# Blocks exchanged on the way back from DRAM instead of transposes on TensorE, earlier loads for the last projection, and fewer mask pieces before the first attention

## The chip, the core and the metric

The kernel runs on one core of a Trainium2 chip. The metric is the device time of one execution in microseconds (us), and lower is better. A core has four engines that matter here: TensorE (PE in the profile, matmuls; PEld is its weight load), VectorE (DVE), ScalarE (ACT), and GpSimd (POOL). SyncE (SP) only issues DMAs in this kernel; POOL issues them too, and a few are issued by ACT. Each of these engines works through its own instructions in a fixed order, and they wait for one another by semaphores. Matmul results go to PSUM, everything else lives in SBUF, and large intermediate arrays go through DRAM.

## The reference

There are N = 3327 nodes with F = 512 features each, and a 0/1 matrix adj of N x N. Four layers follow one another, each as `x = layernorm(x + layer(x, adj))`:

- Layer 0 is graph attention with 8 heads of 64: for every pair (i, j) with adj = 1 the weight is `exp(leaky_relu(f1[i] + f2[j]))`, the weights of a row are divided by their sum, and `h' = attention @ Wh`.
- Layer 1 takes for each node the mean of its first 64 neighbours (a running count along the row of adj cuts the rest off), puts it through a linear map and a leaky ReLU, and adds a second linear map of the node itself.
- Layer 2 is like layer 0 (8 heads of 64), with an ELU at its end.
- Layer 3 is the same with 4 heads of 128.

```
nb_mean = (keep @ X) / max(cnt, 1)             # layer 1, keep: the first 64 neighbours
x = layernorm(x + leaky(X @ W_line.T + b) + where(cnt > 0, leaky(nb_mean @ W_nb.T + b), 0))
attention = softmax(where(adj > 0, leaky_relu(s1[i] + s2[j]), -9e15))   # layers 0, 2 and 3
```

## The kernel before

**Tiles.** The nodes are cut into NT = 26 tiles of P = 128 rows; the last has 127. HALF = 13 tiles are half of them. The mask of adj (transposed) stays in SBUF for the whole kernel as one byte per pair. It is made from 26 x 4 pieces of 128 x 832 int32 (426 KB each, array raw), each turned into bytes by one instruction: on DVE at L558, or on ACT at L557.

**Stages.** In order of time:

1. The first projection (about 0 to 150 us). For each tile of x, `project1` transposes the tile on PE (four 128x128 transposes, L253, into the PSUM tile pt), ACT copies the result to xT (L255), and DVE adds up xsum (L256). `project2` multiplies xT by the weights (pw, L264), ACT copies the head columns (rc, qc, L268) and takes an exp (dc, L265), DVE scales (vt, L270), and a DMA stores v. Beside this, the first `EARLY = 3 * NT + 4 = 82` mask pieces are loaded by SP (L547; the first eight by ACT) and made by DVE. The pieces of the left half of all tiles come first, then the third quarter, then the fourth.
2. The first attention (to about 953 us). For each half of the columns, each of four groups of heads and each tile j, DVE makes the weights t from the mask (L398), ACT makes y from t (L401), and PE multiplies both (po at L421, pd at L373). The remaining mask pieces hang on this loop as `aside`, one step per j: the step loads piece k on SP and makes piece k - 1. Of these pieces, those with k % 5 in (1, 3) are made by ACT, the others by DVE.
3. The first half of layer 1, `sage` (to about 1175 us): the two linear maps of every tile, with z stored in three parts.
4. The mean, the second half of `sage` (to about 1780 us). For each of the 26 output tiles PE adds up 26 x 3 matmuls into acc (L767). Between them PE makes the running counts pk for the next block of two tiles (L735); ACT first puts carried counts into pk (L727) from cy, which POOL loads (L624), and DVE turns pk into the mask kt (L739). When acc is done, DVE and ACT make the finished tile y (L747 to L749, then `norm_rows`: L152 to L161), and SP stores it to the array x2 (L133). The projection of layer 2 for tile y runs inside the matmuls of the following tile, as two jobs: `project1` at step t = 11 and `project2` at t = 17. The tiles y have two buffers, acc has two.
5. The attention of layer 2 (to about 2570 us), then the last projection, in `third` (to about 2722 us): `finish` loads the attention's result h (L126, from hd) and the layer's input xr (from x2), divides (L180), applies the ELU (L185, L191, L192) and normalizes (L152 to L161); then the tile is stored as x3 and goes through `project1` and `project2`. `finish` of a group of two tiles is called one group ahead; h has 6 buffers, and xr has 2. The first group's `finish` runs at the end of the attention before.
6. The attention of layer 3 and the last normalization (to the end).

**What sets the order.** PE's instructions stand in the order in which the program is written. Those of DVE, ACT, POOL and SP are ordered by a scheduler of the build, once and for all; what is wrapped in `keep_in_program_order` stays at its place. A transpose between x2 and xT on DVE works inside blocks of 32 x 32 only; the kernel already uses that at L439, where the following DMAs (L461, hd<-ob) put the blocks at their places in runs of 32 numbers (128 bytes).

Of the kernel before, what the change touches and what calls it, by code (L numbers as in the profile page):

```python
# [7 lines left out]
F32 = mybir.dt.float32  # L8
# [10 lines left out]
P = 128  # L19
# [13 lines left out]
def kernel(  # L33
# [10 lines left out]
    nc = tc.nc  # L44
    N, F = x.shape
    NT = (N + P - 1) // P
    NP = NT * P
    LAST = N - (NT - 1) * P
    FC = F // P
# [20 lines left out]
    ident = const.tile([P, P], F32, name="ident")  # L70
# [45 lines left out]
    x2 = dram.tile([NP, F], F32, name="x2")  # L116
# [45 lines left out]

    def finish_steps(pool, xin, layer, t0, n, hbufs=6, eng=nc.sync):
        H, D = layer.H, layer.D
        ys, xs, steps = [], [], []

        def load():
            for t in range(t0, t0 + n):  # L170
                h = pool.tile([P, F], F32, name="h", bufs=hbufs)
                load_tile(h, hd, t, eng)
                ys.append(h)
                xr = pool.tile([P, F], F32, name="xr")
                load_tile(xr, xin, t, nc.gpsimd)
                xs.append(xr)

        def divide(s):
            h = ys[s]
            nc.vector.tensor_tensor(h.rearrange("p (h d) -> p h d", h=H), h.rearrange("p (h d) -> p h d", h=H),  # L180
                                    rec[:, t0 + s, :H].rearrange("p (h e) -> p h e", e=1).to_broadcast([P, H, D]),
                                    op=ALU.mult)
            if layer.elu:
                e = pool.tile([P, F], F32, name="e")
                nc.scalar.activation(e, h, AF.Exp)  # L185
                xs.append(e)

        def add(s):
            h, xr = ys[s], xs[s]
            if layer.elu:  # L190
                nc.vector.scalar_tensor_tensor(xr, xs[n + s], 1.0, xr, op0=ALU.min, op1=ALU.add)  # L191
                nc.vector.scalar_tensor_tensor(h, h, 0.0, xr, op0=ALU.max, op1=ALU.add)  # L192
            else:
                nc.vector.tensor_tensor(h, h, xr, op=ALU.add)

        steps.append(load)
        for s in range(n):
            steps += [lambda s=s: divide(s), lambda s=s: add(s)]
        steps.append(lambda: norm_rows(pool, ys, t0))
        return ys, steps  # L200

    def finish(*a):
        ys, steps = finish_steps(*a)
        for f in steps:
            f()
        return ys
# [16 lines left out]
    class Layer:  # L223
# [23 lines left out]
            nc.gpsimd.memset(self.sm, 0.0)  # L247


        def project1(self, pool, ps, xt, t):  # L250
            pt = ps.tile([P, FC, P], F32, name="pt")
            for c in range(FC):
                nc.tensor.transpose(pt[:, c, :], xt[:, c * P:(c + 1) * P], ident)  # L253
            xT = pool.tile([P, FC, P], F32, name="xT")
            nc.scalar.copy(xT, pt)  # L255
            nc.vector.tensor_reduce(xsum[:, :, t], xT, AX.X, ALU.add)  # L256
            return xT

# [351 lines left out]
    def sage(first, first_pool, xin, prev, nxt, wsrc, dst):  # L610
        G = 2
        GW = G * P
        blocks = [(b * G, b * GW) for b in range(NT // G)]
        with tc.tile_pool(name="sg_z", bufs=1, reuse_waits="tile") as zp, \
                tc.tile_pool(name="sg_c", bufs=2, reuse_waits="tile") as cyp:

            groups = [(b, t) for b in range(NT // G) for t in range(0, NT, 4)]
# [17 lines left out]
            with tc.tile_pool(name="sa_w", bufs=1, reuse_waits="tile") as wp, \  # L635
# [37 lines left out]
                ahead = first  # L673
                for t0 in range(0, NT, 2):
                    ys, ahead = ahead, finish(fp, xin, prev, t0 + 2, 2, 6, nc.sync if t0 else nc.gpsimd) \
                        if t0 + 2 < NT else None
                    for s, y in enumerate(ys):
                        xT = step1(y)
# [6 lines left out]
            with tc.tile_pool(name="sb_w", bufs=1, reuse_waits="tile") as wp, \  # L685
# [57 lines left out]
                def output(acc, t):  # L743
                    xi = sp.tile([P, F], F32, name="xi")
                    nc.gpsimd.dma_start(out=xi, in_=xid[t * P:(t + 1) * P, :])
                    y = sp.tile([P, F], F32, name="y", bufs=2)
                    nc.vector.scalar_tensor_tensor(y, acc, cnt[:, 1, t:t + 1], bnb, op0=ALU.mult, op1=ALU.add)  # L747
                    nc.vector.scalar_tensor_tensor(y, y, 0.01, y, op0=ALU.mult, op1=ALU.max)
                    nc.vector.scalar_tensor_tensor(y, y, cnt[:, 2, t:t + 1], xi, op0=ALU.mult, op1=ALU.add)  # L749
                    norm_rows(sp, [y], t)  # L750
                    store_tile(dst, y, t, nc.sync)
                    return y

                carry_in(0)
                kts = kept(0, 0) + kept(0, 2)
                jobs = []
                for b in range(len(blocks)):
                    t0, i0 = blocks[b]
                    last = b + 1 == len(blocks)
                    ahead = []  # L760
                    for s in range(G):
                        acc = ps.tile([P, F], F32, name="acc", bufs=2)
                        for t in range(NT):
                            if b == 0 and len(kts) < NT and t % 2 == 0:
                                kts += kept(0, len(kts))
                            for c in range(3):
                                nc.tensor.matmul(acc, kts[t][:, s * P:(s + 1) * P],  # L767
                                                 zs(t, c) if c < 2 else zl[:, t, :],
                                                 start=t == 0 and c == 0, stop=t == NT - 1 and c == 2)
                            if not last and (len(ahead) < 10 and t % 4 == 1 and b > 0 if s == 0 else  # L770
                                             len(ahead) < min(NT, t + 10) and t % 2 == 1):
                                ahead += kept(b + 1, len(ahead))

                            if jobs and (t == 11 or t == 17 and not (last and s == G - 1)):
                                jobs.pop(0)()
                        y = output(acc, t0 + s)
                        held = {}

                        def job1(y=y, t=t0 + s, held=held):
                            held["xT"] = nxt.project1(sp, ps, y, t)  # L780

                        def job2(t=t0 + s, held=held):
                            nxt.project2(sp, bank, wsb, held["xT"], t)
                            if t == HALF - 1:
                                nxt.prepare(sp, 0, "xi", 1)

                        jobs += [job1, job2]
                    kts = ahead
# [5 lines left out]
    def third(first):  # L794
        with tc.tile_pool(name="col3", bufs=1) as cp, tc.tile_pool(name="at_r3", bufs=2, reuse_waits="tile") as rp:
# [3 lines left out]
            with tc.tile_pool(name="p_w", bufs=1, reuse_waits="tile") as wp, \  # L799
                    tc.tile_pool(name="p", bufs=3, reuse_waits="tile") as pp, \  # L800
                    tc.tile_pool(name="p_f", bufs=2, reuse_waits="tile") as fp, \
                    tc.tile_pool(name="p_ps", bufs=2, space=PSUM, reuse_waits="tile") as ps:
                wsb = wp.tile([P, FC, 2, FW + L3.H], F32, name="wsb")
                load_wide(wsb, w3, nc.gpsimd)
                nc.vector.tensor_copy(wsb[:, :, :, FW:], wa[3].rearrange("p c (e h) -> p c e h", e=2))

                def bank(e):
                    return ps.tile([P, 512], F32, name=f"pw{e}")

                pend = None  # L810
                ahead = first
                for t0 in range(0, NT, 2):
                    ys, ahead = ahead, finish(fp, x2, L2, t0 + 2, 2, 6, nc.sync if t0 else nc.gpsimd) \
                        if t0 + 2 < NT else None
                    for s, y in enumerate(ys):
                        t = t0 + s
                        store_tile(x3, y, t, nc.sync)
                        xT = L3.project1(pp, ps, y, t)
                        if pend:
                            L3.project2(pp, bank, wsb, *pend)  # L820
                        pend = (xT, t)
                        if t == HALF + 1:
                            L3.prepare(pp, 0)
                            L3.first_rows = L3.rows(rp, 0, 0)
                            L3.cut(pp, 0)
                L3.project2(pp, bank, wsb, *pend)
                L3.mean(pp, bank, wsb)
# [3 lines left out]
            with tc.tile_pool(name="f3", bufs=2) as fp, tc.tile_pool(name="f4", bufs=1) as gp:  # L831
                g = gp.tile([P, HALF, F], F32, name="g")
# [85 lines left out]
                for qs in (slice(0, cut_), slice(cut_, HALF)):  # L918
# [4 lines left out]
                    for q in reversed(range(qs.start, qs.stop)):  # L923
                        y = g[:, q, :]
# [6 lines left out]
    L0, L2, L3 = Layer(0, 8, False), Layer(2, 8, True), Layer(3, 4, True)  # L931
# [3 lines left out]
    with tc.tile_pool(name="col0", bufs=1) as cp, tc.tile_pool(name="raw", bufs=2) as rawp, \  # L935
# [4 lines left out]
        with tc.tile_pool(name="p_w", bufs=1, reuse_waits="tile") as wp, \  # L940
# [4 lines left out]
                nc.gpsimd.memset(mask[:, NT - 1, :], 0.0)  # L945
            nc.gpsimd.memset(mask[:, :, N:NP], 0.0)
            pieces = [(t, q) for t in range(NT) for q in range(2)] + [(t, q) for q in (2, 3) for t in range(NT)]
            EARLY = 3 * NT + 4
            msteps = mask_steps(rw0, pieces[:EARLY], 5, (), False, 8)

            def load(t):
# [24 lines left out]
            xT = L0.project1(pp, ps, load(0), 0)  # L976
            held = {}
# [5 lines left out]
            for t in range(1, NT):  # L983
                xT = L0.project1(pp, ps, load(t), t)
# [30 lines left out]

        pieces = pieces[EARLY:]
        ends = []
# [65 lines left out]
```

## Time and profile before

Three runs took 3425.46, 3428.16 and 3432.74 us, so the median is 3428.16 us. The profiled execution has a span of 3432.3 us.

| what | busy us | share of the span |
|---|---|---|
| PE | 3295.2 | 96% |
| PE weight loads | 1656.3 | 48% |
| DVE | 2666.0 | 78% |
| ACT | 2374.3 | 69% |
| POOL | 215.1 | 6% |

The share of an engine is a mean over stages which have different limits. A row of the 40 slices shows when an engine is full: each digit is the busy share of one slice of 85.8 us in tenths. In a timeline, a line has the start, the time from the first to the last of the merged instructions, the engine, the line of the kernel, the operation, what it writes and reads, and in brackets how long the engine was idle before it and what ended the wait. Neighbouring instructions of one engine overlap a little, so the cost of one in a full engine is the distance from its start to the next start.

### The profile page before, as it was taken

How to read it: one execution, taken by the hardware profiler on the slowest of the kernel's cores; microseconds unless marked ns; L12 is line 12 of the kernel's file. 1: busy time of each engine (PE TensorE's matmuls, PEld its weight loads, DVE VectorE, ACT ScalarE, POOL GpSimd, SP SyncE). 2: the span in 40 equal slices, each digit the busy share in tenths (PEclk: the TensorE clock that was granted, in tenths of full speed). 3: DMA queues.
4: the chain of work that ended last, by engine and by line, in shares of the span. 5: the costliest groups of instructions: out<-in, count | busy, mean ns of one | idle time of the engine just before them, and what ended most of it. 6: DMA issues, size and time to landing. Idle time of an engine off the chain costs nothing.

```text
span 3432.3 us, 47383 instructions
## 1 busy us (share of the span) xinstructions
PE 3295.2 (96%) x18705; PEld 1656.3 (48%) x18705; DVE 2666.0 (78%) x2571; ACT 2374.3 (69%) x2172; POOL 215.1 (6%) x344
## 2 busy tenths in 40 slices
PE   8799999999999899999989999999998999999997
PEld 7544344444444355555543444444446654455553
DVE  5799999999967443434349999999997766668876
ACT  2388999999943233333338999899997655559985
POOL 3200000000010111111110000000001000000000
PEclk9999999999999999999999999999998999999998
DMA  9732111111043422222220111111116411112211
GB/s 372 279 110 69 51 48 43 53 45 39 26 140 125 127 81 76 71 71 73 70 70 25 43 49 48 53 49 46 32 34 219 160 40 40 42 47 89 82 37 48
DMA packets 225061, 276.62 MB, mean 81 GB/s; under 512 B 45949, under 2 KB 160327, under 8 KB 224840
## 3 DMA queue, kind: packets, MB, share of 16 engines
q1 hardware_dynamic: 192280, 162.21, 14.8%
q0 software_dynamic: 27040, 103.70, 9.6%
q10 hardware_dynamic: 5520, 7.69, 0.7%
q8 instruction: 148, 2.42, 0.3%
q14 instruction: 73, 0.60, 0.1%
HBM read 204.92 MB, written 68.60 MB: 80 GB/s over the span
## 4 chain that ended last, share of the span: by engine, by line
PE 73%; issue 12%; DMA 6%; DVE 4%; ACT 3%; POOL 1%; SPq 0%; POOLq 0%; ACTq 0%; DVEq 0%
PE po L421 49%; PE pd L373 7%; PE acc L767 5%; DVE t L398 3%; PE pw L264 3%; PE pz L655 3%; PE pi L658 3%; DMA raw<-in_adjT_dram 2%; DMA cy<-ctd 2%; ACT y L401 1%; PE pt L449 1%; PE pe L487 1%; DMA r<-rr 0%; POOL cy L624 0%; PE pa L966 0%
## 5 line engine op out<-in xcount | busy, mean ns | idle before, releaser
L398 DVE SCALAR_TENSOR_TENSOR t<-rb,qc,mask 128x1664 f32<-128x1664 f32 x1040 | 1959.0, 1945 | 183.1 <-PE po L421 163.6
L401 ACT ACTIVATE y<-t,bi,sc 128x1664 fp8e4<-128x1664 f32 x1040 | 1770.0, 1766 | 321.7 <-PE pd L373 302.9
L421 PE MATMUL po<-t,vj 128*64 128x448 f32 (+3 forms) x8320 | 1912.8, 521 | 24.4 <-DVE t L398 24.2
L421 PEld LDWEIGHTS po<-t,vj 128*64 128x64 f32 (+1 forms) x8320 | 835.0, 148 | 978.1 <-issue 710.6
L767 PE MATMUL acc<-zs,kt 128*128 128x512 bf16 x1352 | 404.7, 381 | 0.0
L767 PEld LDWEIGHTS <-kt 128*128 128x128 fp8e4 x2028 | 199.3, 98 | 246.0 <-issue 9.6
L264 PE MATMUL pw<-wsb,xT 128*128 128x264 f32 (+1 forms) x1248 | 302.7, 398 | 9.6 <-DVE vt L270 5.1
L727 ACT CAST pk<-cy 128x512 f32<-128x512 bf16 x169 | 98.4, 587 | 287.1 <-DVE kt L739 234.0
L264 PEld LDWEIGHTS pw<-wsb,xT 128*128 128x128 f32 x1248 | 241.5, 197 | 55.9 <-ACT xT L255 6.0
L373 PE MATMUL pd<-y,sden 128*32 128x448 fp8e4 (+1 forms) x4160 | 259.4, 342 | 8.2 <-ACT y L401 8.2
L767 PE MATMUL acc<-zl,kt 128*128 128x512 bf16 x676 | 257.5, 381 | 4.6 <-DMA zl<-zd 4.6
L739 DVE SCALAR_TENSOR_TENSOR kt<-pk,mask 128x512 fp8e4<-128x512 f32 x169 | 116.2, 688 | 108.2 <-PE pk L735 107.8
L373 PEld LDWEIGHTS <-sden 128*32 128x32 bf16 x4160 | 117.5, 96 | 160.3 <-issue 137.6
L270 DVE TENSOR_TENSOR vt<-pw,dc 128x256 f32<-128x256 f32 x156 | 59.2, 416 | 136.7 <-ACT dc L265 129.7
L352 POOL DMA_DIRECT2D rb<-r x40 | 21.3, 533 | 1607.9 <-DVE t L398 1593.4
L268 ACT COPY rc<-pw 128x8 f32<-128x8 f32 (+1 forms) x78 | 12.7, 163 | 151.0 <-PE pw L264 151.0
L655 PE MATMUL pz<-wn,xT 128*128 128x512 f32 x208 | 93.7, 593 | 1.2 <-ACT xT L649 1.2
L658 PE MATMUL pi<-wl,xT 128*128 128x512 f32 x208 | 93.5, 592 | 0.0
L558 DVE TENSOR_SCALAR mask<-raw 128x832 fp8e4<-128x832 int32 (+2 forms) x95 | 56.2, 600 | 45.6 <-DMA raw<-in_adjT_dram 45.2
L747 DVE SCALAR_TENSOR_TENSOR y<-acc,cnt,bnb 128x512 f32<-128x512 f32 x26 | 19.5, 751 | 88.5 <-PE acc L767 88.5
L624 POOL DMA_DIRECT2D cy<-ctd x91 | 67.9, 746 | 289.5 <-ACT pk L727 264.8
L256 DVE TENSOR_REDUCE xsum<-xT 128x4 f32<-128x512 f32 x78 | 53.0, 681 | 39.7 <-ACT xT L255 39.3
(175 smaller groups left out, 1738.4 us busy)
## 6 DMA issues: line engine op xcount, KB each, us to landing
vj<-v SPq DMA_DIRECT2D x312, 128.0 KB
rb<-r POOLq DMA_DIRECT2D x40, 832.0 KB, 4.6
raw<-in_adjT_dram SPq DMA_DIRECT2D x67, 416.0 KB
cy<-ctd POOLq DMA_DIRECT2D x78, 256.0 KB, 3.9
h<-hd SPq DMA_DIRECT2D x61, 256.0 KB
v<-vt SPq DMA_DIRECT2D x50, 256.0 KB
hd<-hb SPq DMA_DIRECT2D x48, 256.0 KB
xr<-x POOLq DMA_DIRECT2D x45, 256.0 KB, 3.1
```

The lines of the kernel that those rows point to most:

```text
L264: nc.tensor.matmul(pw[e][:, :FW + H], xT[:, c, :], wsb[:, c, e, :], start=c == 0, stop=c == FC - 1)
L270: nc.vector.tensor_tensor(vt[:, hs, :], pw[e][:, :FW].rearrange("p (h d) -> p h d", d=D), self.dc[:, t, hs].rearrange("p (h e) -> p h e", e=1)
L373: nc.tensor.matmul(pd[c][32 * kk:32 * kk + 32, :w_], lhsT, rhs, start=(kk, c) not in seen, skip_group_check=final is not None, stop=last a ...
L398: nc.vector.scalar_tensor_tensor(t, rb[k], self.qc[:, j, h:h + 1], mask[:, j, i0:i0 + IW], op0=ALU.max, op1=ALU.mult)
L401: nc.scalar.activation(y, t, AF.Sigmoid, bias=self.bi[:, j, h:h + 1], scale=self.sc[:, j, h:h + 1], saturate=False)
L421: nc.tensor.matmul(po[c][k * D:(k + 1) * D, :z - a_], vj[:, j % 2, k * D:(k + 1) * D], ts[k][:, a_:z], start=j == 0, stop=j == NT - 1)
L624: nc.gpsimd.dma_start(out=cy[:, :n, :], in_=ctd[t:t + n, b * GW:(b + 1) * GW] .rearrange("(o t) i -> o t i", o=1).to_broadcast([P, n, GW]))
L655: nc.tensor.matmul(pz, xT[:, c, :], wn[:, c, :], start=c == 0, stop=c == FC - 1)
L658: nc.tensor.matmul(pi, xT[:, c, :], wl[:, c, :], start=c == 0, stop=c == FC - 1)
L727: nc.scalar.copy(pks[k % 2], carry[b, t // 4 * 4][:, t % 4:t % 4 + 2, :])
L739: nc.vector.scalar_tensor_tensor(kt, pk, NEIGHBOURS, mask[:, t:t + 2, i0:i0 + GW], op0=ALU.is_le, op1=ALU.mult, saturate=False)
L767: nc.tensor.matmul(acc, kts[t][:, s * P:(s + 1) * P], zs(t, c) if c < 2 else zl[:, t, :], start=t == 0 and c == 0, stop=t == NT - 1 and c ...
```

## The change

There are three edits.

**The mean.** A finished tile y (all but the last) is stored as before, and then read back from x2 into a new tile yx by four DMAs on SP. Each takes 32 partitions, and the 32 x 32 blocks come exchanged: block (a, b) of each 128 x 128 square lands where block (b, a) was. `project1` then makes xT by one transpose on DVE, which stays at its place in the program, instead of four transposes on PE and a copy on ACT. The jobs move: `project1` of a tile runs at t = 17 of the following tile, and `project2` at t = 11 of the tile after that.

**The last projection.** The loads of `finish` are issued three groups ahead, its other steps one group ahead as before. h has 10 buffers, xr has 6. The loads of the groups at tiles 2 and 4 are issued before the loop; those of the group at tile 2 stay on POOL for h.

**The masks.** EARLY is 5 * 26 / 2 + 3 = 68 instead of 82, so 36 pieces are made during the first attention, not 22.

```diff
-    def finish_steps(pool, xin, layer, t0, n, hbufs=6, eng=nc.sync):
+    def finish_steps(pool, xin, layer, t0, n, hbufs=6, eng=nc.sync, xbufs=None):
...
-                xr = pool.tile([P, F], F32, name="xr")
+                xr = pool.tile([P, F], F32, name="xr", bufs=xbufs)
...
-        def project1(self, pool, ps, xt, t):
-            pt = ps.tile([P, FC, P], F32, name="pt")
-            for c in range(FC):
-                nc.tensor.transpose(pt[:, c, :], xt[:, c * P:(c + 1) * P], ident)
+        def project1(self, pool, ps, xt, t, blocks=False):
             xT = pool.tile([P, FC, P], F32, name="xT")
-            nc.scalar.copy(xT, pt)
+            if blocks:
+                tc.keep_in_program_order(nc.vector.transpose(xT, xt))
+            else:
+                pt = ps.tile([P, FC, P], F32, name="pt")
+                for c in range(FC):
+                    nc.tensor.transpose(pt[:, c, :], xt[:, c * P:(c + 1) * P], ident)
+                nc.scalar.copy(xT, pt)
...
                     store_tile(dst, y, t, nc.sync)
-                    return y
+                    if t == NT - 1:
+                        return y
+                    yx = sp.tile([P, FC, P], F32, name="yx")
+                    for q in range(4):
+                        nc.sync.dma_start(out=yx[32 * q:32 * q + 32].rearrange("p c (g f) -> p c g f", g=4),
+                                          in_=dst[t * P:(t + 1) * P, :].rearrange("(g a) (c q f) -> q a c g f", g=4, q=4, f=32)[q])
+                    return yx
...
-                            if jobs and (t == 11 or t == 17 and not (last and s == G - 1)):
+                            if jobs and (t == 11 and t0 + s > 1 or t == 17):
                                 jobs.pop(0)()
...
-                            held["xT"] = nxt.project1(sp, ps, y, t)
+                            held["xT"] = nxt.project1(sp, ps, y, t, t < NT - 1)
...
                 ahead = first
+                groups = []
+                def load_group(t0):
+                    if t0 < NT:
+                        groups.append(finish_steps(fp, x2, L2, t0, 2, 10, nc.gpsimd if t0 < 4 else nc.sync, 6))
+                        groups[-1][1].pop(0)()
+                for t0 in (2, 4):
+                    load_group(t0)
                 for t0 in range(0, NT, 2):
-                    ys, ahead = ahead, finish(fp, x2, L2, t0 + 2, 2, 6, nc.sync if t0 else nc.gpsimd) \
-                        if t0 + 2 < NT else None
+                    ys = ahead
+                    load_group(t0 + 6)
+                    if groups:
+                        ahead, steps = groups.pop(0)
+                        for f in steps:
+                            f()
...
-            EARLY = 3 * NT + 4
+            EARLY = 5 * NT // 2 + 3
```

## The prediction

> **What bounds the kernel now.** I read the page's busy shares and slices, then the waits of each of the three places that the change touches, then their timelines.
>
> ```profile
> PE 3295.2 (96%) x18705; PEld 1656.3 (48%) x18705; DVE 2666.0 (78%) x2571; ACT 2374.3 (69%) x2172; POOL 215.1 (6%) x344
> PE   8799999999999899999989999999998999999997
> DVE  5799999999967443434349999999997766668876
> DMA  9732111111043422222220111111116411112211
> ```
>
> PE fills nearly every slice, but the places differ: two slices at the start run the DMA engines full, slices 3 to 11 (first attention) have DVE as full as PE, slices 14 to 21 (the mean) have PE alone, and slice 31 (last projection) has everything a little short.
>
> The mean, a timeline of PE and SP (start, length, engine, line, operation):
>
> ```profile
> 1414.46 0.32 SPq L133 DMA_DIRECT2D x<-y  x1
> 1415.85 0.38 PE L767 MATMUL acc<-zl,kt 128*128 128x512 bf16 x1
> 1416.07 0.60 PE L253 MATMUL pt<-ident,y 128*128 128x128 f32 x4
> 1416.50 0.60 PE L767 MATMUL acc<-zs,kt 128*128 128x512 bf16 x2
> ...
> 1439.70 0.32 SPq L133 DMA_DIRECT2D x<-y  x1
> 1439.73 0.66 PE L253 MATMUL pt<-ident,y 128*128 128x128 f32 x4 [0.37 <-ACT y L161]
> ```
>
> PE goes from one matmul into the next; the four transposes take 0.43 us of its order (1416.07 to 1416.50), and the second group waited 0.37 for its tile. So a matmul taken out here is time won.
>
> The last projection, PE and DVE:
>
> ```profile
> 2633.79 0.69 DVE L180 TENSOR_TENSOR h<-h,rec 128x512 f32<-128x512 f32 x1 [2.90 <-DMA h<-hd]
> 2639.71 3.67 PE L264 MATMUL pw<-wsb,xT 128*128 128x260 f32 x16
> 2646.81 1.03 PE L253 MATMUL pt<-ident,h 128*128 128x128 f32 x4 [3.42 <-ACT h L161]
> 2647.63 5.02 PE L264 MATMUL pw<-wsb,xT 128*128 128x260 f32 x16
> 2684.29 0.69 DVE L191 SCALAR_TENSOR_TENSOR xr<-e,xr 128x512 f32<-128x512 f32 x1 [3.06 <-DMA xr<-x]
> ```
>
> and PE's waits between 2600 and 2722 (in all, times, longest):
>
> ```profile
> PE pt L253 <- ACT h L161: 9.6, 4, 3.4
> ```
>
> DVE stands for a load, and some ten us later PE stands for the tile that the load belongs to: 9.6 us in four waits.
>
> The first stage's end and the first attention, DVE:
>
> ```profile
> 143.29 0.59 DVE L558 TENSOR_SCALAR mask<-raw 128x832 fp8e4<-128x832 int32 x1 [1.40 <-DMA raw<-in_adjT_dram]
> 149.69 7.53 DVE L398 SCALAR_TENSOR_TENSOR t<-rb,qc,mask 128x1664 f32<-128x1664 f32 x4
> 228.93 7.53 DVE L398 SCALAR_TENSOR_TENSOR t<-rb,qc,mask 128x1664 f32<-128x1664 f32 x4
> 236.37 0.59 DVE L558 TENSOR_SCALAR mask<-raw 128x831 fp8e4<-128x831 int32 x1
> 236.88 7.53 DVE L398 SCALAR_TENSOR_TENSOR t<-rb,qc,mask 128x1664 f32<-128x1664 f32 x4
> ```
>
> Before 149.69 DVE waits for mask pieces; after it, it runs without a gap (between 150 and 260 it waits 0.4 us in all). There a mask piece costs 0.51 us of DVE (236.37 to 236.88), and nothing hides it.
>
> **What the Trainium skill says.** "VectorE: DVE Perf Modes", The three transpose paths: VectorE transposes inside 32x32 blocks only, TensorE the full 128x128, into PSUM. That is why blocks must be exchanged on the way back, and why the TensorE way carries a ScalarE copy (L255, 585 ns in the mean). "DMA: Bandwidth & Descriptors", Anatomy of one DMA: some 2 us are fixed, mostly the wait until the last byte has landed. The trace fits: 256 KB of xi land in 2.9 us. The same page, Specifications: below 512 B a transfer doesn't reach full rate. The trace agrees: the 128 B runs of hd<-ob go at 102 to 144 GB/s between 2812 and 2820, where the first stage reads at about 400. "TensorE: Matmul & The Clock Gate", Why this matters for your kernels: idle gaps over about 3 us lower the clock. Above, after 3.42 us, the transposes take 1.03 for 0.60 and the projection 5.02 for 3.67, so such a wait costs some 1.8 us more than itself.
>
> **The change, part by part.**
>
> *Mean.* 25 of 26 tiles lose four transposes: 25 x 0.43 = 10.8 us of PE. PE's waits for y there go too (2.4 us in 7 waits, in PE's waits for this stage). Together 13.2. ScalarE loses 25 copies of 0.585, which aren't on the path. DVE gets a transpose instead of nothing: the nearest row is L439, 583 ns for 128x448 from PSUM, so an estimate of 0.66 us for 128x512, in a stage where DVE is 40% busy; it hides under the matmuls as long as its data is there.
>
> Is it there? Each tile adds four loads on SP, 2048 runs of 128 B. SP first waits until the store has landed (3.8 us, the stores of v of the same size) and then issues four (0.32 to 0.84 each). The 6656 runs of one hd<-ob set moved in 8.4 us (2811.4 to 2819.8), 1.26 ns each, so 2048 take 2.6. That is a write; for a read from DRAM the worst row is cb<-ctd, 3328 elements of two bytes, landed after 11.7 us, so 2048 runs take at most 7.2. With 2 us fixed the blocks arrive 3.8 + 1.5 + 2.6 + 2 = 9.9 us after the store's issue; 14.5 at the upper bound. The store comes 6.6 or 9.9 us after the tile's end (acc read at 1407.85, store 1414.46; 1429.76 and 1439.70). So arrival is 16.5 to 19.8, worst 24.4. The transpose stands, in the built order of DVE, behind the last kt of the next tile and ahead of its first y: PE reaches t = 17 after 17 x 0.65 + 8 x 0.22 + 3.56 (the projection, now at t = 11) = 16.4, and the tile ends at about 22.7 (24 periods of y from 1203.65 to 1749.77). DVE may stand there for up to 3.5 us; behind it are xsum and the next y, which wait for PE anyway. The xT is used only at t = 11 of the tile after. No cost, at the worst bound 1 to 2 us on the y chain, which has 20 us of slack in the second acc.
>
> On SP, the stores of v are behind these loads; nobody waits for them in this stage. On the DMA engines (a quarter busy in the mean) the 2.6 us can hold up a carry load (cy, 3.9 us to land), and PE's order can't pass a pk whose copy is late. ScalarE already waits 51 us for cy, of which 5.6 reach PE. Bounds 0 and 25 x 0.5 = 12 us; I take 1. Mean: -12 us.
>
> *Last projection.* The same loads and arithmetic, issued two groups earlier (xr from 2 to 6 buffers, h from 6 to 10). That takes DVE's waits for h and xr (5.7 + 5.2 us between 2600 and 2722), and with them PE's 9.6 us and about 2.5 of slow clock: at most -12. But the static orders change too. At the start ScalarE now does two exp of the next groups and rc, dc, qc of the first projection ahead of the second group's sqrt, and POOL issues the 1 MB of weights ahead of the second group's loads: PE then waits about 3 us for tile 2 (ScalarE: projection ends, 0.2, table 1.28, 0.29, DVE 0.4, 0.8), and wins 1.5 because the first group gets ready sooner. Also DVE needs 3.85 us a tile (from start to start: 5 x 0.6, 0.67 for vt, 0.2) against PE's 3.95, so it has hardly anything in hand, least where prepare and cut add some 4.5. Bounds -12 and +3; I take -7. On POOL all xr loads now precede the rows of the next attention; they are issued by tile 20, some 25 us before these rows are needed: nothing.
>
> *Masks.* Fourteen pieces leave the first stage: 14 x 0.426 MB at about 390 GB/s = 15 us of DMA, but PE allows less. With mask waits the last tiles take 4.65 us, without them 4.0 (as at 34 to 46 us), for four tiles 2.6; and the pieces and waits between 143.3 and 149.2 vanish from DVE: the first L398 comes at about 143.7 instead of 149.69, -6. In the attention 36 pieces stand instead of 22; by the list of those on ScalarE, 22 instead of 13 are DVE's: 9 x 0.51 = +4.6, all on the path. ScalarE gets 5 x 0.98 more, hidden under DVE (it is 90% busy). The loads are on SP among vj, one per step as before. Sum -1.5, bounds -5 and +4.
>
> Sum -12 - 7 - 1.5 = -20.5 us on the traced 3432.3, that is 3412. The three unprofiled runs are 3425 to 3433 with a median of 3428.16, so **3408 us**.
>
> **Rivals.**
> 1. The last projection wins nothing, since DVE and ScalarE take PE's place as soon as loads are early: for it their load of 3.85 a tile and the order at the start; against it that every long PE wait has a DMA wait before it. Then -13.5: 3415.
> 2. The readback disturbs the carry loads, and PE pays 0.4 us a tile: the mean returns only 2 us. For it: PE's slack for a pk is half a microsecond; against: three quarters of the DMA time are free. Total -10: 3418.
> 3. Slower: the 128 B reads are much slower than the writes of that size. From about 22 us after a tile's end, 12 us after the later stores, DVE holds back kt of the next tile, and PE stops at the second pk. Each us more costs 13 us at first (only every other tile has the later store). The 21.7 us that the change else returns are eaten when the blocks land 1.7 us past that limit, about 14 us after the store's issue, where I expect 9.9; at 15 us the sum is 13 x 3 - 22 = +17: 3445.
> 4. The masks only move: attention +4.6, first stage not earlier, because PE is the bound there. Then the sum is -14: 3414.
>
> **How the numbers follow.** This kernel's three runs spread over 0.2%, so 0.2% (6.9 us) is about what a measurement can tell from no change. Forecast as such 0.52 (3400 to 3416); rivals 1 and 4 together 0.20 (3411 to 3419); rival 2 0.10 (3415 to 3424, half of it inside 0.2%); rival 3 0.09; gains beyond 28 us 0.09. Faster 0.82, same 0.09, slower 0.09. The range 3396 to 3424 leaves out rival 3 and half of the largest gains; the likeliest case's own range is 3400 to 3416.
>
> **What would show it.** Mean: 4 instead of 104 matmuls pt<-y, 25 stream transposes near 0.66 us, the period of y from 22.7 down to about 22.2, no DVE wait for yx beyond 4 us, waits PE pk <- ACT pk still near 6. Last projection: no DVE wait for h or xr after the first groups, PE's wait for h below 5 us. First stage: the first L398 near 144, but the end of the first attention only 1 to 2 us earlier than 953. Wrong would be: long DVE waits for yx, PE waits for pk, or a first projection that stands several times for ScalarE.

## The result and the profile after

The changed kernel takes 3411.38 us (median of 4 runs, 3406.59 to 3413.64) against 3429.25 us on the same chip: a ratio of 0.9946, 95% interval 0.9929 to 0.9964, so 18 us faster. Run again later beside the kernel before it took 3409.40 us, ratio 0.9925 (0.9908 to 0.9943). 3408 was forecast, with 3396 to 3424 as the range.

The traced execution spans 3404.9 us (3432.3 before). The page, engines and slices:

```profile
PE 3279.8 (96%) x18605; PEld 1646.2 (48%) x18605; DVE 2676.6 (79%) x2591; ACT 2363.6 (69%) x2152; POOL 214.8 (6%) x344
PE   8899999999999899999989999999998999999997
DMA  9543111111143433333321011111107311112211
```

PE is 15.4 us less busy and has 100 fewer matmuls: 25 tiles by four transposes. DVE has 10.6 us more. The DMA row at the front went from 9732 to 9543, since the mask pieces come a little later, and in the mean (slices 15 to 20) it rose from 2 to 3: the blocks that are read back.

The mean, timeline of SP and DVE (start, length, engine, line, operation):

```profile
1380.21 0.33 SPq L133 DMA_DIRECT2D x<-y  x1
1382.28 2.60 SPq L761 DMA_DIRECT2D yx<-x  x4
1389.18 0.71 DVE L254 STREAM_TRANSPOSE xT<-yx 128x512 f32<-128x512 f32 x1 [1.67 <-DMA yx<-x]
...
1399.91 0.33 SPq L133 DMA_DIRECT2D x<-y  x1
1403.80 2.60 SPq L761 DMA_DIRECT2D yx<-x  x4
1410.19 0.70 DVE L254 STREAM_TRANSPOSE xT<-yx 128x512 f32<-128x512 f32 x1
```

The first of these tiles had its blocks 9.0 us after its store was issued (DVE stood for them, so 1389.18 is when they came); the second tile's were there when DVE asked, 10.3 us after the store. DVE's waits over the whole mean (in all, times, longest):

```profile
DVE xT L254 <- DMA yx<-x: 10.2, 10, 1.8
```

Over those ten tiles the blocks came 7.7 to 9.0 us after the store's issue. The waits don't reach PE: among its own waits from 1175 to 1765 none is for this transpose. In the last projection, PE's waits and the start of its timeline:

```profile
PE pt L258 <- ACT h L161: 4.5, 2, 3.6
```

```profile
2580.08 0.66 PE L258 MATMUL pt<-ident,h 128*128 128x128 f32 x4 [3.63 <-ACT h L161]
2580.58 5.36 PE L268 MATMUL pw<-wsb,xT 128*128 128x260 f32 x16
2586.21 3.67 PE L268 MATMUL pw<-wsb,xT 128*128 128x260 f32 x16
```

Of the long waits for h one is left, the one that the new order makes at the start (3.63, and 1.7 more in the matmuls after it, 5.36 for 3.67). The other 0.9 us of the 4.5 are one short wait. The first attention begins here:

```profile
142.13 7.54 DVE L402 SCALAR_TENSOR_TENSOR t<-rb,qc,mask 128x1664 f32<-128x1664 f32 x4 [0.98 <-PE pw L290]
```

What ends the idle time is now PE's last matmul of the projection, and no mask piece.

**The stages over all traces.** I measured the same landmarks in the trace of every kernel: the first t (start of the first attention), the first `h<-h,rec` after it, the first and last `y<-acc` of the mean, the first transpose of the last projection and the first `po` of the last attention. The kernels below `after` are described under the experiments. Lengths in us:

| Kernel | start of first attention | first attention | mean | last projection |
|---|---|---|---|---|
| before | 149.69 | 803.51 | 563.39 | 130.69 |
| mean_alone | 147.07 | 804.78 | 548.15 | 133.88 |
| shift_alone | 145.97 | 804.31 | 559.46 | 133.43 |
| proj_alone | 145.04 | 804.66 | 563.26 | 122.34 |
| masks_alone | 142.71 | 811.26 | 563.55 | 131.88 |
| after | 142.13 | 807.05 | 546.47 | 124.08 |
| after_again | 142.31 | 808.14 | 548.67 | 123.10 |
| no_mask_edit | 144.46 | 805.33 | 548.69 | 124.79 |
| early_56 | 138.78 | 812.63 | 548.74 | 123.63 |
| no_readback | 142.91 | 808.54 | 547.17 | 124.03 |
| slot_14 | 143.40 | 807.73 | 548.67 | 123.05 |
| slot_11 | 142.90 | 809.26 | 725.03 | 123.58 |
| sage_blocks | 143.97 | 809.86 | 546.95 | 124.63 |
| sage_free | 141.66 | 809.12 | 546.20 | 123.92 |

The table is worth more than a comparison of the first two traces. Five programs with the same first stage (82 pieces) begin their first attention anywhere from 144.46 to 149.69, so the trace of before was the latest of five. The 7.6 us that two traces seem to show there are half a matter of the draw: from the mean of these five (146.4) to the mean of the eight with 68 pieces (142.7) it is 3.7 us.

### The profile page after: what moved, and what is told of

Read it like the earlier page. It is cut to its first block, busy times and chain, and to the rows that moved or that the text cites. A ratio compares the mean times of both kernels' runs of the same rounds, so it can differ in the third digit from the quotient of the medians.

```text
span 3404.9 us, 47272 instructions
## 1 busy us (share of the span) xinstructions
PE 3279.8 (96%) x18605; PEld 1646.2 (48%) x18605; DVE 2676.6 (79%) x2591; ACT 2363.6 (69%) x2152; POOL 214.8 (6%) x344
## 3 DMA queue, kind: packets, MB, share of 16 engines
q1 hardware_dynamic: 245080, 168.77, 16.3%
## 4 chain that ended last, share of the span: by engine, by line
PE 80%; DVE 6%; issue 6%; DMA 5%; ACT 3%; POOL 0%; ACTq 0%; POOLq 0%; SPq 0%; DVEq 0%
PE po L425 49%; PE acc L778 11%; PE pd L377 7%; PE pw L268 4%; DVE t L402 4%; DMA raw<-in_adjT_dram 3%; PE pz L659 3%; PE pi L662 3%; ACT y L405 1%; PE pt L453 1%; PE pk L739 1%; PE pe L491 1%; DMA cy<-ctd 1%; DVE mask L562 0%; DMA cb<-ctd 0%
```

## Experiments

**1. The three parts, each alone.** Each is the kernel before with one part of the diff. For the mean:

```
-            nc.scalar.copy(xT, pt)                      # after four TensorE transposes of y
+            tc.keep_in_program_order(nc.vector.transpose(xT, xt))    # xt: y read back in blocks
-            if jobs and (t == 11 or t == 17 and not (last and s == G - 1)):
+            if jobs and (t == 11 and t0 + s > 1 or t == 17):
```

> The kernel before with the edit of the mean alone (readback in exchanged blocks, VectorE's transposes, the later job slots). Theory: between the first y and the last y the trace of the changed kernel was 16.9 us shorter, and this edit alone brings all of it: 13 to 17 us faster, about 3413 to 3416 us, with the last y some 17 us earlier in the trace and the last projection still 130 us long. Rival A: the readback disturbs the carry loads and the edit pays less than the transposes that leave TensorE: 3 to 7 us faster. Rival B: the 16.9 us came from other conditions that the mask or projection edits made: under 3 us.

Measured: ratio 0.9949 (0.9935 to 0.9964), 17.5 us. The mean is 15.2 us shorter than in the trace of before, and the projection is not shorter (133.88 for 130.69). Rivals A and B fall.

For the last projection:

```
-  ys, ahead = ahead, finish(fp, x2, L2, t0 + 2, 2, 6, ...)
+  ys = ahead
+  load_group(t0 + 6)          # h 10 buffers, xr 6
```

> The kernel before with the edit of the last projection alone (loads three groups ahead, ten h and six xr buffers). Theory: the stretch from the first transpose of the projection to the first matmul of the last attention falls from 130.7 to about 124 us and the kernel is 6 to 7 us faster, about 3422 us. Rival: the attention that follows takes it back (it was 2 us longer in the trace of the changed kernel), or the projection is bound by its engines and not by its loads: under 2 us.

Measured: ratio 0.9965 (0.9952 to 0.9977), 12 us; the interval reaches down to 8. PE's waits for h in the projection:

```profile
PE pt L253 <- ACT h L161: 3.6, 1, 3.6
```

Four waits of 9.6 us in all have become the one at the start. Of DVE's waits for the two loads, those for xr (5.2 us in before, between 2600 and 2722) are gone. Of those for h (5.7 us in four) two are left, of 2.2 us in all here and of 4.3 in the changed kernel, and little of them reaches PE. The stage is 8.3 us shorter than in the trace of before; over the traces of the table, it takes 132.5 us without this edit (four) and 123.7 with it (ten).

A part of that goes back just ahead of the landmark. From the last `po` of the attention before to the first transpose of the projection it is 19.3 us without the edit (19.1 to 19.6) and 21.1 with it (20.6 to 21.7). PE there, in before and then in the changed kernel:

```profile
2587.68 0.47 PE L449 MATMUL pt<-ident,ob 128*128 128x128 f32 x1 [0.72 <-ACT hb L453]
2592.09 1.97 PE L253 MATMUL pt<-ident,h 128*128 128x128 f32 x8 [3.93 <-ACT h L161]
```

```profile
2566.68 0.48 PE L453 MATMUL pt<-ident,ob 128*128 128x128 f32 x1 [3.93 <-ACT hb L457]
2569.33 1.97 PE L258 MATMUL pt<-ident,h 128*128 128x128 f32 x8 [2.17 <-ACT h L161]
```

The first group is ready sooner, but the attention's own copy hb on ACT comes later. From that last `po` to the first `po` of the last attention the edit is worth 6.9 us (151.8 to 144.9). The last attention and normalization take back nothing (710.9 us without, 710.8 with). So the loads were what bound it, and by the stages the gain is the 6 to 7 us that were expected; the timing says more.

For the masks (`EARLY = 3 * NT + 4` to `5 * NT // 2 + 3`, 82 to 68):

> The kernel before with 68 mask pieces in place of 82 ahead of the first attention, nothing else. Theory: the first attention starts 7.5 us earlier and takes 3.5 us longer, because 14 more pieces lie in a stretch that VectorE and ScalarE nearly fill: 3 to 5 us faster, about 3425 us. Rival A (the prediction's own sum): 1.5 us faster. Rival B: pieces only move, and the attention takes back all of it: within 1 us.

Measured: ratio 0.9994 (0.9986 to 1.0003), so between 5 us faster and 1 slower: no gain that the timing can tell from nothing. The stages speak for rival B: the start comes earlier, and the attention takes it back (experiment 5).

**2. What the mean is made of.** The same later slots, but TensorE goes on transposing y and nothing is read back:

```
-            if jobs and (t == 11 or t == 17 and not (last and s == G - 1)):
+            if jobs and (t == 11 and t0 + s > 1 or t == 17):
```

> The kernel before with only the job slots of the mean moved (transposes of a tile at step 17 of the next tile and its matmuls at step 11 of the one after); TensorE still transposes y from SBUF and nothing is read back. Theory: the mean's 16.9 us are about 11.3 us of transposes (25 tiles by 0.43 to 0.49 us) and about 5.6 us of TensorE's wait for y at step 11, which the later slot removes; so this kernel is 4 to 7 us faster, the wait of pt for ScalarE's y is near zero, and the pair period is near 44.4 us. Rival A (as the prediction priced it): the wait was worth 2.4 us over all tiles, so 1 to 3 us faster. Rival B: the slot does nothing, and all 16.9 us are the transposes' (they cost more than their rows say): within 1 us.

Measured: ratio 0.9971 (0.9960 to 0.9981), 10 us by the timing, but 3.9 us by the stage that it changes. In the trace the rest lies in the start of the first attention (145.97 for 149.69), which this edit doesn't touch. The timing's interval (7 to 14 us) leaves out 3.9; why it gives more than the stage stays open, and I rest on the stage. 3.9 lies between the theory (4 to 7) and rival A (1 to 3). PE's groups in the mean, of before and then of this kernel:

```profile
L253 PE MATMUL pt<-ident,y 128*128 128x128 f32 x100 | 15.7, 279 | 3.0 <-ACT y L161 2.4
```

```profile
L258 PE MATMUL pt<-ident,y 128*128 128x128 f32 x100 | 15.0, 273 | 0.0
```

The wait is gone. So the later slot gives 3.9 us. Taking the transposes out gives 10.7 to 13.3 more (559.46 to between 546.20 and 548.74 in the seven traces that hold the whole of this edit), 11.8 to their mean of 547.7, against 25 x 0.43 = 10.8. By the timing the difference of the two kernels is 7.5 us, with intervals of 4 and 5 us: too wide to tell these apart.

**3. Is the readback hidden?** The changed kernel without the four loads of a tile; VectorE transposes y itself.

> The changed kernel without the four loads a tile: VectorE transposes y itself within its 32x32 blocks, so what the second layer projects is not the transposed tile; the readback in exchanged blocks is left out, all else stays. Theory: the readback is wholly hidden: the stretch from the first to the last y stays near 548.6 us, and the time is within 2 us of the changed kernel. Rival 2 of the prediction (the loads disturb the carry loads, 0.04 to 0.4 us a tile): 1 to 10 us faster than the changed kernel.

Measured: ratio 0.9932 (0.9918 to 0.9946), 3409.31 us; the mean takes 547.17. That is inside what the kernels with the readback show (546.20 to 548.74). 100 loads of 128 B runs cost nothing that can be seen here, and nothing near the 10 us of the prediction's second rival, which falls.

**4. The deadline of the blocks.** The changed kernel with VectorE's transposes earlier, first by three steps (`t == 17` to `t == 14`), then in the slots of before (`t == 11 or t == 17 and not (last and s == G - 1)`).

> The changed kernel with VectorE's transposes of the tile before at step 14 of the mean's 26 instead of step 17, some 2.4 us earlier. In the changed kernel's trace the blocks were there about 9 us after the store's issue, and VectorE stood at most 1.8 us for them. Theory: now VectorE stands 1 to 4 us at most tiles, and TensorE, which can run ahead by two pk, hardly stands: within 4 us of the changed kernel. Rival 3 of the prediction (each us in which VectorE is held past the slack costs a us of TensorE at 24 tiles): 20 to 60 us slower.

Measured: ratio 0.9927 (0.9915 to 0.9940), the same as the changed kernel. DVE's waits in the mean:

```profile
DVE xT L254 <- DMA yx<-x: 13.7, 11, 2.2
```

Three steps cost DVE 3.5 us in all (it stood at 11 tiles, where the theory had it stand at most of them), and the mean takes 548.67: PE loses nothing.

> The changed kernel with VectorE's transposes at step 11 of the next tile and the projection's matmuls at step 17, which are the slots of the kernel before. By the trace of the changed kernel step 11 comes some 8 us after a tile's end, its y is stored 8 to 9 us after it, and the blocks land some 9 us after that. Theory (rival 3's mechanism, reached from the other side): VectorE stands up to 9 us at every tile with kt behind it, TensorE stops at the second pk and again for xT at step 17, some 3 to 5 us a tile: 60 to 120 us slower than the changed kernel. Rival: TensorE's hold on pk and the kept kt of ten tiles carry it over: under 15 us slower.

Measured: ratio 1.0431 (1.0412 to 1.0451), 149 us slower than before and 174 slower than the kernel without readback beside it. DVE's timeline, PE's timeline, and PE's waits from 1199 to 1930:

```profile
1398.77 0.71 DVE L254 STREAM_TRANSPOSE xT<-yx 128x512 f32<-128x512 f32 x1 [4.74 <-DMA yx<-x]
```

```profile
1399.63 6.24 PE L268 MATMUL pw<-wsb,xT 128*128 128x264 f32 x16 [5.03 <-DVE xT L254]
```

```profile
PE pw L268 <- DVE xT L254: 118.2, 25, 5.7
PE pk L739 <- ACT pk L731: 1.6, 3, 1.0
```

Every tile stands some 4.7 us for xT, and the sixteen matmuls after a wait take 5.9 us on average (5.2 to 6.7, 6.24 in the line above) where the changed kernel's took 3.72 (at 1401.51). 118 + 25 x 2.2 = 173 us, near the 174. The profile also shows the clock that TensorE was granted, as a share of full speed: from 1399.6 to 1402 it is 0.50, and over the mean of the changed kernel 1.00. My theory named the wait for xT, but missed the slow clock and so put the loss at 60 to 120; the place that rival 3 names (PE at the second pk) is wrong: PE waited 1.6 us for pk.

This kernel moves two things: the transposes to step 11, and the matmuls that use them to step 17 of the same tile. The blocks came at 1398.77, and PE, which stood before its step 17, went on 0.86 us later. So PE waited for the load through VectorE, and it would have to wait for it at that step wherever the transpose stood. What transposes at step 11 cost when the matmuls stay a tile later was not run.

**5. The masks again, in the changed kernel.** The whole once more, the whole with 82 pieces, and with 56 (`EARLY = 2 * NT + 4`).

> The changed kernel itself once more, so that the parts can be compared with the whole on one chip. The three parts alone gave ratios of 0.9949 (mean), 0.9965 (last projection) and 0.9994 (masks) to the kernel before. If they add, the whole stands at 0.9908, about 31 us faster than before. If part of it is lost in the combination, or the parts' ratios were high draws, it stays near the 0.9946 of its first run (18 us).

> The changed kernel with 82 mask pieces first, as before; so the mean's and the last projection's edits together. Theory (masks only move: over six traces the first attention starts 4.5 us earlier with 68 pieces and takes 4.9 us longer): within 2 us of the changed kernel. Rival (the landmarks of the first two traces, which gave the mask edit 4 us): 3 to 5 us slower than the changed kernel.

> The changed kernel with 56 mask pieces first in place of 68: the mask edit nearly doubled. Theory (what the first stage gives, the attention takes): first attention starts 4 us earlier still and takes 4 us longer, total within 2 us of the changed kernel. Rival A (the first stage gives 0.54 us a piece, the attention takes 0.25): 3 to 4 us faster. Rival B (the attention's engines are full by now, each further piece costs more than 0.5 us there): 3 to 6 us slower.

Measured, on one chip: 0.9925 (0.9908 to 0.9943) with 68 pieces, 0.9923 (0.9909 to 0.9936) with 82, 0.9932 (0.9917 to 0.9946) with 56. No difference can be told. The start of the first attention in mean_alone (82), masks_alone (68) and early_56:

```profile
147.07 5.67 DVE L402 SCALAR_TENSOR_TENSOR t<-rb,qc,mask 128x1664 f32<-128x1664 f32 x3
```

```profile
142.71 7.54 DVE L398 SCALAR_TENSOR_TENSOR t<-rb,qc,mask 128x1664 f32<-128x1664 f32 x4 [0.98 <-PE pw L286]
```

```profile
138.78 7.54 DVE L402 SCALAR_TENSOR_TENSOR t<-rb,qc,mask 128x1664 f32<-128x1664 f32 x4 [0.98 <-PE pw L290]
```

With fewer pieces the attention starts earlier each time, by about 0.3 us a piece, and takes as much longer or a little more: 804.5 us (the five traces with 82), 808.9 (the eight with 68), 812.6 (the one with 56). So the theory holds at three sizes. As for the whole: the parts' gains sum to 31.6 us, the whole gave some 26 here (0.9925). The intervals (5, 4 and 3 us on the parts, 6 on the whole) are too wide to call that a loss, and the parts share one set of runs of the kernel before, so that an error of that set stands in the sum three times. Summed by stages it is 15.7 for the mean, 6.9 for the projection and 0.7 lost on the masks, 22 in all.

**6. The same idea one stage earlier.** In the stage ahead of the mean PE is full as well, so I tried the exchange there for tiles 6 to 25, finished a group earlier:

```
+                    if yx is not None:
+                        xT = sp.tile([P, FC, P], F32, name="xT")
+                        tc.keep_in_program_order(nc.vector.transpose(xT, yx))
+                        return xT
...
-    ys, ahead = ahead, finish(fp, xin, prev, t0 + 2, 2, 6, ...)
+    ys = queue.pop(0)                                    # the group after it is stored to yd here
+    queue.append(finish(fp, xin, prev, t0 + 4, 2, 7, ...))
...
+    yxs[t0 + 2 + s] = back(t0 + 2 + s)                   # four loads, as in the mean
...
```

Two buffer counts change with it, which no run separates: the stage's tile r1 has one buffer, and h has seven.

> The changed kernel with the same exchange in the stage ahead of the mean: tiles 6 to 25 are finished one group earlier, stored once more, read back in exchanged blocks and transposed by VectorE; TensorE keeps the transposes of tiles 0 to 5. There TensorE goes from matmul to matmul too (30.0 us of 30 between 985 and 1135) and four transposes take 0.44 us of its order; VectorE works 20 to 22 us of 30 and would get 0.70 a tile more. Theory (a matmul taken out of a full TensorE stream is time won as long as the blocks arrive): 20 x 0.44, so the stretch from the end of the first attention to the first y of the mean falls from about 251 to 242 us, and the kernel is 7 to 10 us faster than the changed one, about 3401 us. Rival A: the extra finish of a group ahead and the waits for blocks (VectorE has only some 2 us a tile free) give it back: within 3 us. Rival B: stores and loads on the queue of the stage's other transfers hold up z3 and xi, VectorE stands for their buffers: 5 to 20 us slower.

Measured: ratio 1.0102 (1.0088 to 1.0116), 36 us slower than before and some 61 slower than the changed kernel (no_readback beside it took 3409.31): a loss that is larger than any that I had written down. PE's waits (980 to 1240) and its timeline:

```profile
PE pz L663 <- DVE xT L651: 46.6, 8, 6.3
```

```profile
1074.23 5.45 PE L663 MATMUL pz<-wn,xT 128*128 128x512 f32 x8 [6.02 <-DVE xT L651]
1079.52 3.60 PE L666 MATMUL pi<-wl,xT 128*128 128x512 f32 x8
```

DVE has no wait for the blocks in this stage. Its order has the transposes of two tiles (at 1073.46) right behind the finish of the next group (1070.31 to 1073.44). Without the pin the build puts them elsewhere:

```
-                        tc.keep_in_program_order(nc.vector.transpose(xT, yx))
+                        nc.vector.transpose(xT, yx)
```

> The kernel of the run before (exchange in the stage ahead of the mean for tiles 6 to 25) with VectorE's transposes no longer held behind the whole finish of the group to come: in the built order the transposes of tile k+2 now stand between the first and the last VectorE step of tile k, where before those of k and k+1 stood after the last step of k-1. In the run before TensorE stood 46.6 us in 8 waits for xT and lost its clock. Theory: that order was the whole loss, so those waits vanish and the gain that was meant comes out: the stretch from the end of the first attention to the first y of the mean about 242 us (251 in the changed kernel), the kernel 7 to 10 us faster than the changed one, about 3401 us. Rival A: VectorE's share (0.70 us more a tile, of some 2 us free) or the blocks' arrival is the next bound: within 3 us of the changed kernel. Rival B: the queue of stores and loads holds up z3 and xi: slower by 3 to 20 us.

Measured: ratio 1.0003 (0.9993 to 1.0014), so no faster than before and some 25 us slower than the changed kernel. PE's waits (950 to 1222) and a place of its timeline:

```profile
PE pz L663 <- DVE xT L651: 16.3, 6, 3.5
PE pk L759 <- ACT pk L751: 11.8, 3, 9.8
```

```profile
1081.38 5.40 PE L663 MATMUL pz<-wn,xT 128*128 128x512 f32 x8 [3.50 <-DVE xT L651]
```

The waits for xT fell from 46.6 to 16.3 us but did not vanish: once in two tiles a transpose still stands behind finishing steps that come in one run on DVE (1072.88 to 1080.02 ahead of the transpose at 1080.62). Some 7 us of slow clock follow them. PE's wait for pk at this stage's end is longer, 11.8 us where the changed kernel run again has 5.0, but its wait for zl there (a stored part of z) is shorter, 1.1 for 5.0. The stage takes 270.9 us where it takes 249.6 and 251.4 in the changed kernel. The order was a part of the loss and not the whole. Whether an order written out by hand would give the 8.8 us was not tried. No version that I ran beats the changed kernel; those with 82 and 56 pieces and slot_14 tie with it.

## Why the prediction was right, point by point

- **The total.** 3408 was forecast and 3411 and 3409 came. The sum on the trace was -20.5; the two timings give -18 and -27, the stages -22. That the total fits to 3 us is in part luck: the timings lie 9 us apart, and the mean's gain was put too low while the masks' was put too high. The chances of the cases, added up, give 0.86 for faster and 0.05 for the same, not 0.82 and 0.09.
- **Mean, -12: right in mechanism, two terms mis-sized.** Measured -15.7 (563.4, the mean of three traces in the table, to 547.7, the mean of the seven that hold the whole of this edit). The transposes were put at 10.8 and gave some 11.8. The wait for y was put at 2.4, read from PE's waits; taking it away gave 3.9. The 1 us for disturbed carry loads was not there. Of the 5.6 us that PE was said to wait for pk, one wait of 4.5 stands before the first y; within the mean it is 1.0 in before and 0.7 after.
- **The readback.** Arrival was put at 9.9 us after the store's issue and was 7.7 to 9.0 at the ten tiles where DVE stood for it. The store's landing was taken as 3.8; the loads were issued 2.1 to 4.3 us after the store, 3.6 in the middle. From the first of the four loads to the landing 6.1 were taken (1.5 + 2.6 + 2) and 4.6 to 6.9 measured. The fixed 2 us in it had been seen in the trace on a load that GpSimd issues; no run shows that term apart for SP's loads. DVE's stand was put at up to 3.5 us and was at most 1.8. The transpose was estimated at 0.66 us and took 0.70. The Trainium skill, "VectorE: DVE Perf Modes", The three transpose paths, says that this path stays inside 32x32 blocks; the 0.70 is this case's own number.
- **Last projection, -7: the size came, its terms only in part.** The stage itself gives -8.8 (132.5 to 123.7), and 1.8 go back ahead of it: -6.9. -12 was the most, and some 5 were taken off for the start and for DVE as the next bound. The start cost what was said (3.63 and 1.7), and the first group was ready 1.8 us sooner (2.17 for 3.93, with 1.5 said). That hb would come 3.2 us later (3.93 for 0.72) was not foreseen. DVE didn't become the bound: after the start PE waited 0.9 us for h in all (4.5 - 3.6).
- **Masks, -1.5: in size nothing.** DVE's price in the attention was right: +4.6 was said and 4.4 measured. The -6 at the start was the step that failed. It was read off one trace, whose start (149.69) is the latest of five of the same program part; the others lie between 144.46 and 147.07. The start after the change was put at 143.7, and the eight traces lie between 141.66 and 143.97; but from mean to mean the gain is 3.7. Rival 4 gave the right sum (nothing) with the wrong reason: the start did come earlier.
- **Rival 1** fell with proj_alone, **rival 2** with no_readback, **rival 3** with the landing itself (at most 9.0 us where DVE stood for it; the rival needs about 14) and with slot_14: three steps less slack still cost nothing. slot_11 shows what a late landing costs, though at the matmuls that use xT and not at pk.
- **Slow clock.** The Trainium skill, "TensorE: Matmul & The Clock Gate", Part 1, speaks of windows of about 3.4 us that run freely. Here waits of 3.50, 3.63, 5.03 and 6.02 us were followed by matmuls that took 5.40, 5.36, 6.24 and 5.45 in place of 3.6 to 3.7. But in sage_free one wait of 3.51 (at 1155.47) was followed by 3.70, and two waits of 2.17 by 3.70 (at 1099.25) and by 5.40 (at 1136.04): no sharp limit shows here.

## What to carry to other kernels

Where one engine runs without a gap, a piece of work taken off it is worth its own step in that engine's order (0.43 us of transposes, 25 times), as long as what replaces it arrives before the instruction order asks for it. The slot in which its result is used can cost more than the work itself: the same readback cost nothing with the matmuls a tile later, and 174 us with them at step 17 of the same tile, before the blocks had come. And before a gain at one landmark is counted, the landmark's spread over several traces of the same code must be known; work that is moved between two stages has to be summed over both. The same holds for a wait at the edge of a stage: the projection's 8.8 us are 6.9 when the end of the stage before is counted in.

## What was not expected of the hardware

- In slot_11 a wait of 4.7 us on PE in each tile made the mean 7.1 us a tile longer (725.03 for 547.7, 25 tiles): some 2.2 us of it in the sixteen matmuls that follow.
- Four loads of 512 runs of 128 B each take 2.6 us of SP's queue to issue (557 to 647 ns each) and moved beside full matmul streams without a measurable effect on PE (the mean takes 547.17 us without them and 546.20 to 548.74 with them).
- Programs that are the same in their first stage differ there by up to 5.2 us from trace to trace (144.46 to 149.69), while the mean repeats within 0.3 us in the kernels that keep the old code of it (563.26, 563.39, 563.55) and within 2.5 us in those with the new one (546.20 to 548.74).
